# A two-layer sparse graph kernel: the last full block of the sorted rows goes without slots

## The chip, the cores and the metric

The kernel runs on one core of a Trainium2 chip. The metric is the device time of one execution in microseconds (us), the median of several runs. A profile is one execution recorded by the hardware profiler; its times are counted from the first instruction. Five engines work side by side, each through its own queue in order: TensorE (PE; its weight loads are listed as PEld), VectorE (DVE), ScalarE (ACT), GpSimd (POOL) and SyncE (SP). In this kernel GpSimd issues the gathers and scatters of rows, SyncE the plain loads.

## The reference

There are 2708 nodes with 1024 features in f32 and an adjacency matrix of zeros and ones, which is sparse: a node has few neighbours, and the expected number falls with the node's index.

```python
# layer 0: attention over the neighbours
q = x @ W_q.T + b_q;  k = x @ W_k.T + b_k;  v = x @ W_v.T + b_v
z = (q @ k.T) / sqrt(1024) * adj
z = where(z == 0, -10000, z)
x1 = layernorm(x + relu(softmax(z, axis=1) @ v))
# layer 1: a sum over the neighbours
out = layernorm(x1 + adj @ (x1 @ weight) + bias)
```

Two consequences matter here. A row without neighbours has all its scores at -10000, so its softmax is uniform and its attention output is the mean of v over all nodes, the same row for every such node. And in layer 1 such a row gets no neighbour sum: its output is layernorm(x1 + bias).

## The kernel before, in words

The kernel never forms the dense products. With M = W_q.T W_k it computes y = x M once per node (`y_block`), so that a score is a dot product of a y row with an x row. Since the rows of softmax sum to one, softmax @ v is (softmax @ x) @ W_v.T + b_v: for every row the kernel gathers its neighbours' x rows, mixes them into one row r, and multiplies r by W_v. Layer 1 does the same with x1 and `weight`. A small flag at the end says whether a row had more neighbours than its block has room for; if so, a dense path follows that computes everything again.

Rows are sorted by their number of neighbours, in two families (the first 1024 nodes and the other 1684), and cut into 22 blocks of 128 rows: blocks 0 to 7 and 8 to 21. Block 21 has only 20 rows. `SLOTS` says how many neighbours a block has room for: block 20 has one, block 21 none. Block 0 shares its work with a "hub" of extra slots. Blocks with one slot (18, 19, 20, the list `single`) go through `attend_one`: a mean row from `mean_rows` is overwritten by the one neighbour where there is one (L890), and a second piece of the job computes the score for the flag. The other blocks go through `attend`, one score (L813) and one accumulation (L870) per slot. Blocks with no slot are in `last`; they need no r, and `project_mean` multiplies the mean of x by W_v.

Layer 0 runs by a written list `steps`: "y" steps (y of one block), "v" steps (the projection of one block, `project`, L739) and "p" steps (the projection of two blocks as a pair). A pair is cut into quarters and done in seven half-size products instead of eight (`pair_products`, L999): VectorE builds four sums of the transposed blocks (`turn_pair`, L988 to L991) and evacuates partial results (L1011), and four differences of the weight quarters (L1136 to L1139) are made in place before the first pair. Before a product the rows r are transposed on TensorE (`flip`, L716) and copied by ScalarE (L717). After it, `finish0` or `finish_pair` adds the residual x, normalizes and scatters the rows to x1 (L703).

What VectorE works on meanwhile comes from the lists `jobs` and `late_jobs`: a planner keeps a credit in microseconds and runs the next job when there is credit, when a coming step needs its rows, or while block 0 is still in the list from step 15 on. Late jobs, those of the second family and block 7, wait until all y are done. Three buffers hold rows r.

Layer 1 runs over `units`. Its order of code is: turn the next unit's rows (`turn1`), fetch its residuals (`gather_x1`: ScalarE copies the bias into an xr buffer, L1251, and a gather adds x1 rows to it), issue the row gathers of the unit three ahead (`sum_rows`, L349 on GpSimd, L1238 and L1241 on VectorE), then the products (`work1`). The first unit, (20,), is a single block; the other ten are pairs. After unit 2 the blocks in `last` are fetched and finished without a product, by `finish1` with half sums on ScalarE (L1260). The xr buffers number three for the first block of a unit and the blocks in `last`, two for the second blocks. Before the first product the differences of the layer's weight quarters are made (L1304 to L1307).

The tile framework orders each engine's queue by priority, which follows the order of the code unless a block of code is marked urgent, and by readiness in its own model; the engine then works through that queue in order.

Of the kernel before, what the change touches and what calls it, by code (L numbers as in the profile page):

```python
# [20 lines left out]
P = 128  # L21
# [4 lines left out]
HUB = 32  # L26
# [4 lines left out]

SLOTS = [15, 11, 8, 6, 5, 4, 3, 2] + [13, 5, 4, 4, 3, 3, 3, 2, 2, 2, 1, 1, 1, 0]
ALONE = [8]
# [47 lines left out]
def sparse_part(ctx, tc, x, xT, adj, wqT, wkT, wvT, bq, bk, bv, w1, b1, out):  # L81
    nc = tc.nc
# [28 lines left out]
    with es:  # L111
# [608 lines left out]
        def flip_shares(shares, rT=None):  # L720
# [11 lines left out]
            return rT  # L732

        def project(rT, w):
            po = []
# [9 lines left out]
        def project_mean(rT, w):  # L745

            acc = p_o.tile([P, HALF], F32, name="po")
            with tc.high_priority(URGENT):
# [8 lines left out]
            for h in range(NH):  # L757
                acc = p_o.tile([P, HALF], F32, name="po")
                for g in range(h * G // NH, (h + 1) * G // NH):
                    k = g * D // G - h * HALF  # L760
                    put = nc.tensor.matmul(acc[:HUB, k:k + D // G], ident[:, g * HUB:(g + 1) * HUB], quarters,
                                           start=True, stop=True)
                po.append(acc)
            products.append(put)
            return po

# [296 lines left out]
        def finish_pair(pair, ts):  # L1063
            for k, (b, t) in enumerate(zip(pair, ts)):
# [9 lines left out]
                else:  # L1074
# [9 lines left out]
        jobs = [6, 5, 4, 3, 2, 2, 1, 1, "hub", "hub", 0, 0, 0]  # L1084
        pairs = [(7, 20), (19, 18), (17, 8), (16, 11), (15, 10), (9, 14), (13, 12)]
        late_jobs = [7, 20, 8, 19, 18, 8, 17, 8, 16, 11, 15, 10, 20, 9, 14, 19, 13, 12, 18]
        late = set(late_jobs)
        jobs, late_jobs = jobs + late_jobs, len(late_jobs)
        steps = [("y", 8), ("y", 9), ("y", 10), ("y", 11), ("y", 12), ("v", 6), ("y", 13), ("v", 5), ("y", 14), ("v", 4), ("y", 15), ("v", 3),
                 ("y", 16), ("v", 2), ("y", 17), ("y", 18), ("y", 19), ("y", 20), ("y", 21)]  # L1090
        steps += [("v", b) for b in [1, 0] + last] + [("p", pair) for pair in pairs]

# [14 lines left out]

        def turn0(b):
            if b in last:
                rT = hp.tile([P, DC, HUB], F32, name="mean", tag="y0T")  # L1110
                nc.scalar.copy(rT, xbT.unsqueeze(2).to_broadcast([P, DC, HUB]))
                return rT
# [6 lines left out]
        for i, (kind, b) in enumerate(steps):  # L1119
# [20 lines left out]
            for c in [c for st in steps[i:i + 3] for c in blocks_of(st) if not (left_y and c in late)]:  # L1140
                while c not in done0 and c not in got and c != 0:
                    credit -= run_job()
            while 0 in jobs and i >= 15:
                credit -= run_job()
# [75 lines left out]

        units = [(20,), (19, 18), (17, 16), (15, 1), (14, 2), (7, 8), (9, 3), (4, 10), (6, 0), (5, 11), (12, 13)]
        assert sorted(last + [b for unit in units for b in unit]) == list(range(NB))
# [421 lines left out]
```

## Time and profile before

| What | us |
|---|---|
| time before, median of 3 runs | 1066.83 (1064.39 to 1071.95) |
| profiled execution, from its first to its last instruction | 1065.8 |
| TensorE busy in it | 1007.5 |
| VectorE busy in it | 850.6 |
| GpSimd busy in it | 493.0 |
| ScalarE busy in it | 425.4 |
| end of the last product of layer 0 | 748.9 |
| first transposes of layer 1 | 760.7 |
| end of the last product of layer 1 | 1048.5 |

The profiled execution's time is given by its span alone, and it lies among the three timed runs. A line such as `L999 PE MATMUL po<-w,rT 128*128 128x512 f32 x8` reads: line 999 of the kernel, TensorE, a matmul that writes tile po from w and rT, a 128 by 128 stationary operand and 512 moving columns, eight records. Behind a row stands the time that the engine stood idle before it and what released it. Busy time of TensorE is modelled by the profiler and consecutive matmuls overlap, so starts are a better ruler than lengths.

### The profile page before, as it was taken

Reading aid. Unit: us, or ns where it says so; the run is one execution under the profiler, and the core shown is the slowest. Engines: PE = TensorE matmul, PEld = TensorE weight load, DVE = VectorE, ACT = ScalarE, POOL = GpSimd, SP = SyncE. Lnnn points to the kernel's source line nnn. Section 1 sums busy time; section 2 is a strip of 40 time slices with the busy share of each in tenths; the row PEclk is TensorE's granted clock in tenths of the full one; section 3 lists DMA queues with packets and bytes.
Section 4 is the critical chain, followed back from the end, with each engine's and each line's share of the span. In section 5 each row is a group of like instructions: output and inputs, shape, how many; then the busy total and the mean of one; then the engine's idle time right before and its main releaser. Section 6 shows DMA issues by size and latency. Waiting matters only on the chain.

```text
span 1065.8 us, 10216 instructions
## 1 busy us (share of the span) xinstructions
PE 1007.5 (95%) x2849; PEld 475.1 (45%) x2849; DVE 850.6 (80%) x1831; ACT 425.4 (40%) x894; POOL 493.0 (46%) x397
## 2 busy tenths in 40 slices
PE   7999999999988999999999999999589999999993
PEld 6444444444443444444545444444334444454441
DVE  8799999995287879999399999974678878896432
ACT  4688788422042332224424344332422363333321
POOL 1000140057654545526166666611577777787300
PEclk9999999999999999999999999999799999999997
DMA  9555458565887656796533777726589689979701
GB/s 363 184 205 204 167 207 290 160 216 168 292 250 253 200 181 203 236 331 201 175 114 96 239 247 258 260 95 210 151 286 262 201 274 324 282 221 323 192 40 42
DMA packets 90963, 229.20 MB, mean 215 GB/s; under 512 B 18411, under 2 KB 40395, under 8 KB 88189
## 3 DMA queue, kind: packets, MB, share of 16 engines
q0 software_dynamic: 48768, 148.05, 43.5%
q1 hardware_dynamic: 42128, 80.41, 21.9%
q8 instruction: 24, 0.39, 0.2%
q14 instruction: 43, 0.34, 0.1%
HBM read 219.61 MB, written 33.68 MB: 238 GB/s over the span
## 4 chain that ended last, share of the span: by engine, by line
PE 24%; DVE 12%; issue 5%; DMA 5%; POOL 3%; ACT 1%; POOLq 0%; DVEq 0%; ACTq 0%
PE po L999 21%; DVE r L870 3%; DMA g<-x_d,tabs 3%; DVE junkv L813 3%; DVE t L1011 1%; DMA yg<-y_d,tabs 1%; POOL g L349 1%; POOL xr L343 1%; PE tr L716 1%; PE po L739 1%; PE tr L729 1%; ACT junks L775 1%; DVE t L1069 1%; DVE r L1241 1%; DMA out_dram<-xr,tabs 0%
## 5 line engine op out<-in xcount | busy, mean ns | idle before, releaser
L319 PE MATMUL po<-m_sb,xt 128*128 128x512 f32 x672 | 292.1, 593 | 3.9 <-DVE yo L323 3.9
L319 PEld LDWEIGHTS po<-m_sb,xt 128*128 128x128 f32 x672 | 126.4, 190 | 160.1 <-issue 151.9
L813 DVE SCALAR_TENSOR_TENSOR junkv<-yg,g 128x1024 uint8<-128x1024 f32 x109 | 133.0, 1220 | 34.1 <-DMA g<-in_x_dram,tabs 16.7
L349 POOL DMA_INDIRECT g<-in_x_dram,tabs x86 | 110.7, 1288 | 72.3 <-DVE r L870 20.4
L999 PE MATMUL po<-t,s_all 128*128 128x512 f32 x272 | 124.3, 600 | 2.7 <-DVE xr L1011 2.7
L1241 DVE SCALAR_TENSOR_TENSOR r<-g,valid,r 128x1024 f32<-128x1024 f32 x77 | 98.6, 1281 | 19.1 <-DMA g<-x_d,tabs 18.3
L609 PE MATMUL po<-wk_o,wq_o 128*128 128x512 f32 x256 | 110.5, 592 | 0.0
L739 PE MATMUL po<-wv,rT 128*128 128x512 f32 x224 | 99.4, 602 | 3.6 <-DVE pr L855 3.0
L775 ACT ACTIVATE junks<-t,lnm 128x1024 uint8<-128x1024 f32 (+1 forms) x41 | 47.0, 1147 | 123.7 <-DVE lnm L773 95.2
L349 POOL DMA_INDIRECT g<-x_d,tabs x67 | 77.6, 1158 | 22.7 <-issue 12.8
L563 POOL DMA_INDIRECT tab_d<-rec,pos_i x22 | 27.1, 1230 | 130.0 <-DVE pos_i L552 123.6
L870 DVE SCALAR_TENSOR_TENSOR r<-g,pr,r 128x1024 f32<-128x1024 f32 x64 | 81.8, 1279 | 5.9 <-ACT r L882 4.6
L999 PE MATMUL po<-w,rT 128*128 128x512 f32 x192 | 86.4, 599 | 0.0
L332 ACT ACTIVATE junka<-xt 128x128 f32<-128x128 f32 x176 | 53.8, 306 | 76.1 <-PE po L319 57.5
L999 PEld LDWEIGHTS po<-t,s_all 128*128 128x128 f32 x272 | 51.9, 192 | 68.5 <-issue 61.9
L788 ACT ACTIVATE t<-t,nmr,rstd 128x1024 f32<-128x1024 f32 (+1 forms) x41 | 50.0, 1237 | 81.2 <-DVE nmr L787 81.0
L224 DVE MAX8 few<-a 128x8 f32<-128x75 f32 (+3 forms) x132 | 79.2, 618 | 0.0
L609 PEld LDWEIGHTS po<-wk_o,wq_o 128*128 128x128 f32 x256 | 48.3, 190 | 59.3 <-issue 59.1
L999 PE MATMUL po<-w,s_all 128*128 128x512 f32 x160 | 72.1, 592 | 0.0
L221 DVE SCALAR_TENSOR_TENSOR a<-a,iota 128x2708 f32<-128x2708 f32 (+1 forms) x22 | 65.2, 2963 | 5.4 <-ACT junk L220 5.4
L739 PEld LDWEIGHTS po<-wv,rT 128*128 128x128 f32 x224 | 42.8, 193 | 57.6 <-issue 56.8
L717 ACT COPY rT<-tr 128x512 f32<-128x512 f32 x80 | 43.1, 586 | 56.1 <-PE tr L716 56.1
(350 smaller groups left out, 1524.6 us busy)
## 6 DMA issues: line engine op xcount, KB each, us to landing
a<-in_adj_dram SPq DMA_DIRECT2D x21, 1354.0 KB, 5.9
xt<-in_xT_dram SPq DMA_DIRECT2D x21, 512.0 KB, 5.2
y_d<-yo SPq DMA_DIRECT2D x21, 512.0 KB, 6.1
g<-in_x_dram SPq DMA_DIRECT2D x21, 512.0 KB, 8.0
wq_i<-in_wqT_dram SPq DMA_DIRECT2D x8, 512.0 KB, 8.7
wk_i<-in_wkT_dram SPq DMA_DIRECT2D x8, 512.0 KB, 10.9
wv<-in_wvT_dram SPq DMA_DIRECT2D x16, 256.0 KB, 6.0
w<-in_w_dram SPq DMA_DIRECT2D x4, 1024.0 KB, 7.8
```

The source lines that it names most:

```text
L221: nc.vector.scalar_tensor_tensor(a[:n], a[:n], 1.0, iota[:n], op0=ALU.is_equal, op1=ALU.mult)
L224: nc.vector.max(few[:n, i * 8:(i + 1) * 8], a[:n, cuts[i]:cuts[i + 1]])
L319: put = nc.tensor.matmul(po, xt[:, c, :], m_sb[c // 2][:, c % 2, k0:k1], start=(c == 0), stop=(c == DC - 1))
L332: put = nc.scalar.activation(junka, xts[b][:, c, :], AF.Copy, accum_out=xs[:, c, b:b + 1])
L349: nc.gpsimd.indirect_dma_start(out=dst[:n], out_offset=None, in_=src, in_offset=bass.IndirectOffsetOnAxis(ap=at, axis=0), bounds_check=N - ...
L609: nc.tensor.matmul(po, wq_o[i // 2][:, o, i % 2 * P:(i % 2 + 1) * P], wk_o[:, o, hs], start=(o == 0), stop=(o == DC - 1))
L739: put = nc.tensor.matmul(acc, rT[:, c, :], w[c // 4][h][:, c % 4, :], start=(c == 0), stop=(c == DC - 1))
L775: nc.scalar.activation(junks[:n], t[:n], AF.Square, bias=nm[:n], accum_out=vs[:n])
L813: nc.vector.scalar_tensor_tensor(junkv[:n], yg[:n, :D], scale, xg[:n], op0=ALU.mult, op1=ALU.mult, accum_out=s)
L870: nc.vector.scalar_tensor_tensor(r[:n], xg[j][:n], pr[:n, j:j + 1], r[:n], op0=ALU.mult, op1=ALU.add)
L999: put = nc.tensor.matmul(acc, a[:, k], w[:, k], start=start and k == 0, stop=stop and k == DC // 2 - 1, skip_group_check=True)
L1241: put = nc.vector.scalar_tensor_tensor(r[:n], xg[:n], ok[:n, j:j + 1], r[:n], op0=ALU.mult, op1=ALU.add)
```

## The change

Block 20 gets no slot and joins block 21 in `last`. In layer 0 both take their rows from one product of the mean: `project_mean` now spreads the mean over all 128 partitions instead of 32, and the second call returns the same banks. Block 1, which had a "v" step of its own, takes block 20's place in the pairs: the first pair is (1, 19) and the second (7, 18). The job list loses block 20's two pieces, and the jobs of block 0 are forced one step earlier, since its projection is now the first "v" step after the y's. In layer 1 the unit (20,) goes, ten pairs stay, and both blocks 20 and 21 are finished after unit 2 without a product.

```diff
-SLOTS = [15, 11, 8, 6, 5, 4, 3, 2] + [13, 5, 4, 4, 3, 3, 3, 2, 2, 2, 1, 1, 1, 0]
+SLOTS = [15, 11, 8, 6, 5, 4, 3, 2] + [13, 5, 4, 4, 3, 3, 3, 2, 2, 2, 1, 1, 0, 0]
...
+        mean_po = []
...
         def project_mean(rT, w):
+            if mean_po:
+                return mean_po[0]
...
-                    put = nc.tensor.matmul(acc[:HUB, k:k + D // G], ident[:, g * HUB:(g + 1) * HUB], quarters,
+                    put = nc.tensor.matmul(acc[:, k:k + D // G], ident[:, g * HUB:g * HUB + 1].to_broadcast([P, P]), quarters,
                                            start=True, stop=True)
                 po.append(acc)
             products.append(put)
+            mean_po.append(po)
             return po
...
-        pairs = [(7, 20), (19, 18), (17, 8), (16, 11), (15, 10), (9, 14), (13, 12)]
-        late_jobs = [7, 20, 8, 19, 18, 8, 17, 8, 16, 11, 15, 10, 20, 9, 14, 19, 13, 12, 18]
+        pairs = [(1, 19), (7, 18), (17, 8), (16, 11), (15, 10), (9, 14), (13, 12)]
+        late_jobs = [19, 7, 8, 18, 8, 17, 8, 16, 11, 15, 10, 9, 14, 19, 13, 12, 18]
...
-        steps += [("v", b) for b in [1, 0] + last] + [("p", pair) for pair in pairs]
+        steps += [("v", b) for b in [0] + last] + [("p", pair) for pair in pairs]
...
         def turn0(b):
+            if b in last[1:]:
+                return None
...
-            while 0 in jobs and i >= 15:
+            while 0 in jobs and i >= 14:
                 credit -= run_job()
...
-        units = [(20,), (19, 18), (17, 16), (15, 1), (14, 2), (7, 8), (9, 3), (4, 10), (6, 0), (5, 11), (12, 13)]
+        units = [(19, 18), (17, 16), (15, 1), (14, 2), (7, 8), (9, 3), (4, 10), (6, 0), (5, 11), (12, 13)]
```

## The prediction

> **What bounds the kernel now.** First the page's head and busy times: TensorE is busy 95% of the span, VectorE 80%.
>
> ```profile
> span 1065.8 us, 10216 instructions
> PE 1007.5 (95%) x2849; PEld 475.1 (45%) x2849; DVE 850.6 (80%) x1831; ACT 425.4 (40%) x894; POOL 493.0 (46%) x397
> ```
>
> A share over the whole span hides the stages, so I cut the span where TensorE's work changes: 523 to 565 single blocks of layer 0, 565 to 749 its seven pairs, 749 to 784 the change of layers with the single unit of block 20, 784 to 1049 the ten pairs of layer 1. Columns: busy us of each engine, granted clock, DMA share, GB/s.
>
> ```profile
> 523.00:565.00 42.00, 41.45 (x208) 22.47 (x207) 35.09 (x62) 17.15 (x39) 19.59 (x14) 1.00 0.38 118
> 565.00:749.00 184.00, 180.28 (x488) 83.38 (x485) 158.33 (x365) 68.98 (x129) 94.86 (x68) 1.00 0.62 203
> 749.00:784.00 35.00, 21.45 (x74) 12.10 (x74) 21.16 (x27) 11.29 (x17) 23.91 (x17) 0.80 0.69 187
> 784.00:1049.00 265.00, 260.02 (x713) 122.48 (x711) 189.15 (x342) 93.96 (x160) 171.43 (x137) 0.99 0.74 232
> 540.00:703.00 163.00, 159.48 (x504) 74.73 (x503) 159.95 (x333) 63.15 (x119) 99.29 (x70) 1.00 0.59 195
> ```
>
> TensorE hardly stands still in either pair stage, but from 540 to 703 VectorE is as full (159.95 of 163). Then TensorE's timeline across the change of layers (start, length, line, what, count, idle before):
>
> ```profile
> 745.31 3.60 PE L999 MATMUL po<-t,rT 128*128 128x512 f32 x8
> 760.69 1.94 PE L716 MATMUL tr<-ident,r 128*128 128x128 f32 x8 [11.67 <-DVE r L1238]
> 762.46 2.07 PE L999 MATMUL po<-w,rT 128*128 128x512 f32 x2
> 767.54 13.04 PE L999 MATMUL po<-w,rT 128*128 128x512 f32 x30
> 782.99 1.06 PE L716 MATMUL tr<-ident,r 128*128 128x128 f32 x8 [1.54 <-DVE r L1241]
> 783.89 7.03 PE L999 MATMUL po<-w,rT 128*128 128x512 f32 x16
> 793.59 5.40 PE L999 MATMUL po<-t,s_all 128*128 128x512 f32 x8 [2.67 <-DVE xr L1011]
> ```
>
> Two records make one f32 matmul of the code, and groups of 8 start 3.43 us apart, so 0.429 us a record: a block alone is 16 matmuls = 32 records = 13.7 us, a pair 56 records = 24.0 us, and 8 transposes 0.9 us (590.47 to 591.34). Block 20 alone fills 762.5 to 780.4. Last the chain of waits where the small last block is finished in layer 1:
>
> ```profile
> 861.80 4.99 DMA out_dram<-xr,tabs
> 866.87 1.04 ACT xr L1251
> 869.86 0.66 PE tr L716 x4
> ```
>
> A residual buffer xr comes free only when the last block's scatter has landed; ScalarE's next copy stands in its queue behind that, the copies of turned rows behind it, and TensorE loses 1.63 us.
>
> **What the Trainium skill says.** "TensorE: Matmul & The Clock Gate", Part 1: an idle window of about 3.4 us halves the array's clock, and about 3.4 us of work restores it. The trace agrees: after the 11.67 us gap the granted clock is 0.53 from 761 to 767, 1.00 after. "SBUF — State Buffer", Who interferes with whom: a VectorE instruction with two SBUF inputs contends with GpSimd reads. The trace fits: beside the weight differences the xr gathers at 761.71 and 766.85 took 2.55 and 3.22 us, 1.16 at 679.51 without such a neighbour. "Perfetto Trace Analysis", Identifying the Most-Contended Engine: matmul busy time is a poor measure; hence I count start-to-start.
>
> **Part by part.**
>
> *Layer 0, TensorE.* Pairs stay seven: block 1 takes 20's place. Block 1's own step goes: 32 x 0.429 = 13.7 us; of transposes one block's net, 0.9 us. The mean's first product stays (64 records, 3.6 us). Its spreading keeps 8 records of 256 columns (1.91 us), with full instead of narrow outputs; weight loads may grow from 106 to 190 ns, 8 x 0.08 = 0.7 us at most and beside the matmuls, so I take 0. The second last block reuses the banks. Sum: -14.6 us.
>
> *Layer 0, the others.* Gone for block 20: one score (1.22 + 0.08), the mask (0.2), one accumulation (1.28), so 2.8 us of VectorE; a mean-row copy (1.15) and one block's turned copies (2 x 0.59) of ScalarE; three GpSimd gathers (some 1.3 us each), not its xr gather nor its scatter. A step of two adds, a relu-sum and a norm is only exchanged between blocks 1 and 20: 0. Block 1's row buffer, one of three, is held longer; VectorE has enough else to do, so 0, at most one row stream of 3 us.
>
> What is late next is VectorE. The last turned rows are ready at 703.2 and their pair starts at 724.7; block 8's are ready at 605.4, and its pair starts at 617.6, where the first 6.9 us need the partner alone. TensorE comes 14.6 us sooner, VectorE's row work only 2.8, minus the evacuations of half a pair more (about 5 us) that now fall before it. So block 8 is late by about 14.6 - 12.2 - 6.9 + 2.2 + 4 = 2 us, the 4 being its transposes, copies and sums. The four weight differences (L1136 to L1139, 2.2 us each) now meet the finishing of three blocks, about 2 us; and block 19's result buffer waits for block 0's scatter, 0 to 3 us, with VectorE's queue behind that add. I take 4 us of new stalls in all, bounds 0 and 11.8 (nothing but VectorE's 2.8 is gained). The third job of block 0 is issued a step sooner, but VectorE is full there (39.8 of 40 us in 460 to 500) and the work the same: 0, within 2 us either way. Layer 0: **-10.6** (between -14.6 and -2.8).
>
> *Change of layers.* The 11.67 us gap stays: the last scatter and the first gathers do not change. Then unit (19, 18) is first: block 19's transposes take block 20's place at 760.7, block 18's rows block 19's place (landed by 763.2); the first two products need block 19 alone, so with 3.8 us of transposes at the slow clock the products start by about 764.5. Its products started at 783.9: 19.4 us removed, of which 13.7 are block 20's products. What they covered comes out: the differences L1304 to L1307 are 4 x 2.2 = 8.9 us and the four sums 2.7 us, of which two differences and two sums must precede the third product. From 760.5 that is about 5.8 us of VectorE plus the wait for rows, against 7 to 8 us of products at the half clock. The residual is asked for later in GpSimd's queue, behind six row gathers at 1.3 us instead of three: from 757.6 it is issued at 766 and lands 5.7 later at 772, and one more add goes before the third product: about 2 us. The old stall in that place was 2.67 and falls away with that pair's old position, so I charge 2.
>
> *Layer 1, row gathers.* GpSimd issues all the time (14 per 20 us) and loses one gather, 1.3 us; block 20's moved no rows. If TensorE is some 18 us sooner, do rows arrive? Rows ready against start of their pair: (15, 1) 803.6 and 840.1; (14, 2) 825.7 and 865; (7, 8) 855.9 and 893; (9, 3) 884.6 and 919; (4, 10) 904.9 and 945; (6, 0) 956.0 and 975.9; (5, 11) 975.7 and 1000. Only (6, 0), with the hub, has under 20: 19.9 less 5 for its transposes, so 18 - 1.3 - 15 = about 2 us of stall.
>
> *Layer 1, the zero blocks.* Block 20 now ends like 21: a bias copy (1.05), two half sums (2 x 0.80), a norm on ScalarE, a gather and a scatter. The sums are new, 1.6 us of ScalarE beside matmuls; VectorE drops 2 x 0.77 + 0.69 + 0.75. But 20 and 21 take two of three xr buffers, so a unit's residual can be asked for only as its forerunner's leaves or block 20's scatter lands. Copy 1.05 + issue 1.5 + landing 5.7 = 8.3 us against 6.9 us until the third product needs it: 1.4, and for the next unit again; GpSimd's and ScalarE's queues stand behind those waits as at 866.87. I take 4, bounds -1.6 (the present stall gone) and 12. Layer 1: -19.4 + 2 + 2 + 4 = **-11.4**.
>
> **Sum.** -10.6 - 11.4 = -22.0 on the profiled execution's 1065.8 us span gives 1043.8. Its time lies 1.0 below the median 1066.83; from the median it is **1045**.
>
> **Rivals.**
> - *Everything hidden.* No new stall: -14.6 - 19.4 = -34, 1033. For it: rows lie 20 to 40 us ahead. Against: VectorE full from 540 to 703. Chance 0.12.
> - *VectorE holds layer 0* and the xr buffers cost their worst: -2.8 - (19.4 - 4 - 8) = -10.2, 1057. For it: 98% busy there, four stalls of TensorE on row results in 673 to 704. Against: results come 20 us before their pair. Chance 0.19.
> - *The two zero blocks block layer 1.* If block 20's scatter stands in GpSimd's queue behind two units' row gathers (2 x 13 x 1.3 = 34 us), and the next unit's residual waits for it, that wait less 6 us of lead is 28; with 5 of landing it takes 33 out: 1045 + 33 = 1078. It decides against the change from a wait of 22 us. Against: the buffer of the forerunner comes free anyway. Chance 0.08.
> - *The change does not do what it says:* a row of block 20 with a neighbour would raise the flag and run the dense path, at least three projections of 22 blocks, 3 x 22 x 13.7 = 904 us more. In the reference's adjacency 164 of the last 1684 rows are empty and blocks 20 and 21 need 148. Chance 0.01.
>
> **How the numbers follow.** The forecast, 1045, gets 0.60, between 1037 and 1053. The range takes in both neighbours, 1032 to 1059. 1% is 10.7 us, about what a measurement here can tell from no change: under 1056.2 lie the forecast, the hidden case and a third of the VectorE case: 0.78; within 1% the rest of that case: 0.13; above it the two last: 0.09.
>
> **What would show it.** Right: the first pair of layer 0 starts near 551 instead of 565, the first pair products of layer 1 come 4 us after the first transposes, and TensorE's count falls from 2849 records to 2769 (64 of products, 16 of transposes). Wrong: TensorE idle before transposes on row accumulations (L870) above 12 us in the pair stage, waits for a scatter of xr above 10 us in layer 1, or matmuls queued behind transposes whose rows are not there.

## The result, and the profile after

The changed kernel takes 1076.73 us (median of four runs, 1073.67 to 1084.39), the kernel before, timed beside it, 1065.61 (1063.28 to 1071.95). The ratio is 1.010, 95% interval 1.0066 to 1.0134: about 1% slower, where 1045 and a gain of 2% were forecast. The time lies above the range (1032 to 1059).

The head and busy times of the changed kernel's page, which answer the first lines of the prediction:

```profile
span 1071.9 us, 10026 instructions
PE 987.5 (92%) x2769; PEld 467.0 (44%) x2769; DVE 842.8 (79%) x1820; ACT 422.9 (39%) x893; POOL 493.0 (46%) x393
```

TensorE has 2769 records, the number forecast, and 20 us less of busy time. The work is gone; the time is not. The span is 6.1 us longer, so TensorE is 26 us longer not busy. (The profiled run of the changed kernel is the fastest of its four, so the span shows less of the loss than the medians.)

TensorE's timeline of the changed kernel, its stalls over 1.5 us behind 504 (start, length, line, what, count, idle before and what ended it). Lines have moved by a few: L1004 is the old L999, L1016 the old L1011, L875 the old L870, L1245 and L1248 the old L1238 and L1241, L1258 the old L1251.

```profile
504.97 2.43 PE L319 MATMUL po<-m_sb,xt 128*128 128x512 f32 x4 [2.48 <-DMA xt<-in_xT_dram]
...
570.38 2.84 PE L1004 MATMUL po<-wv,s_all 128*128 128x512 f32 x6 [1.70 <-DVE lnm L776]
575.50 3.70 PE L1004 MATMUL po<-t,s_all 128*128 128x512 f32 x8 [2.28 <-DVE t L1016]
594.95 1.94 PE L716 MATMUL tr<-ident,r 128*128 128x128 f32 x8 [6.29 <-DVE r L875]
...
760.85 1.94 PE L716 MATMUL tr<-ident,r 128*128 128x128 f32 x8 [13.85 <-DVE r L1245]
...
839.00 6.28 PE L1004 MATMUL po<-t,s_all 128*128 128x512 f32 x8 [4.98 <-DVE xr L1016]
892.29 5.24 PE L1004 MATMUL po<-t,s_all 128*128 128x512 f32 x8 [4.16 <-DVE rstd L790]
960.96 0.60 PE L729 MATMUL tr<-to_h,part 128*128 128x32 f32 x2 [9.57 <-DVE part L1248]
```

Of these only the one at the change of layers was there before (11.67 us). Before, the stage up to the pairs had no wait for a slab, the pairs of layer 0 no stall over 1.3 us, and TensorE reached the transposes of block 0, in the unit that also carries the hub, without a pause:

```profile
955.35 1.02 PE L999 MATMUL po<-w,rT 128*128 128x512 f32 x2
956.21 0.40 PE L729 MATMUL tr<-to,r 128*128 128x96 f32 x2
```

VectorE's last accumulation for that unit ended at 956.1:

```profile
953.49 2.60 DVE L1241 SCALAR_TENSOR_TENSOR r<-g,valid,r 128x1024 f32<-128x1024 f32 x2
```

The slack was 0.1 us: TensorE and the rows came level. Behind the new stall the clock is low too: the small transposes of the hub start 0.85 us apart instead of 0.45. "TensorE: Matmul & The Clock Gate", Part 1, of the Trainium skill says that an idle window of about 3.4 us halves the clock; 9.57 us of idleness and these starts agree. The low clock lasts longer than the 3.4 us of work that the prediction took from the same page: the granted clock is 0.50 up to 969 and 1.00 from 971, so it takes some 9 us here, and it took about 6 us after the change of layers.

The windows of the layer-1 stage, from the first row gather to those transposes, in the kernel before and in the changed one (length, busy us and count of each engine, granted clock, DMA share, GB/s):

```profile
757.60:956.40 198.80, 189.43 (x528) 90.91 (x529) 161.16 (x252) 69.48 (x119) 157.18 (x123) 0.97 0.83 257
```

```profile
755.60:960.90 205.30, 179.68 (x488) 84.81 (x488) 158.05 (x250) 71.70 (x123) 159.25 (x122) 0.93 0.81 249
```

Read the fifth pair, GpSimd. Between two of its DMA issues lie 0.30 us, so before it spends 157.2 + 123 x 0.30 = 194.1 of 198.8 us issuing, and after 159.3 + 122 x 0.30 = 195.9 of 205.3. Its queue is full in this stage in both kernels, though the whole span shows it 46% busy; the rest is 4.7 us of waits before and 9.4 after. In GpSimd's account 4.7 us more of waits and 1.8 of issue, net, make up the 6.5 us by which the stage grew. "Perfetto Trace Analysis", What "DMA-bound" means, of the Trainium skill has the case: the sequencer track of the issuing engine is solid with DMA slices. The trace agrees once the 0.30 us between the slices are counted; only, it shows in this stage and not in the share of the whole span.

GpSimd's timeline of the changed kernel, where its queue waits and where the hub's rows are fetched:

```profile
895.35 0.91 POOL L703 DMA_INDIRECT out_dram<-xr,tabs  x1 [4.88 <-ACT xr L793]
...
913.32 0.99 POOL L349 DMA_INDIRECT g<-x_d,tab  x1 [0.30 <-issue]
...
935.08 1.02 POOL L349 DMA_INDIRECT g<-x_d,tab_h  x1 [0.30 <-issue]
...
956.68 1.63 POOL L343 DMA_INDIRECT xr<-x_d,tabs  x1 [0.31 <-issue]
```

Block 0's 15 gathers by `tab` and the hub's 11 by `tab_h` run from 913 to 954 without a residual gather (L343) between. In the kernel before the hub's ran from 898 to 913, then came two scatters, two residual gathers and three gathers for block 6, then block 0's.

VectorE and ScalarE of the changed kernel, the waits at the head of their queues, and VectorE's last six accumulations for the hub:

```profile
569.63 0.69 DVE L1016 TENSOR_TENSOR t<-po,bias_bc 128x512 f32<-128x512 f32 x1 [4.71 <-DMA x_d<-t,tabs]
...
831.27 2.48 DVE L1248 SCALAR_TENSOR_TENSOR r<-g,valid,r 128x1024 f32<-128x1024 f32 x2 [5.48 <-DMA g<-x_d,tabs]
...
889.55 1.28 DVE L1248 SCALAR_TENSOR_TENSOR r<-g,valid,r 128x1024 f32<-128x1024 f32 x1 [3.87 <-DMA g<-x_d,tabs]
...
918.88 1.28 DVE L1248 SCALAR_TENSOR_TENSOR r<-g,valid,r 128x1024 f32<-128x1024 f32 x1 [2.32 <-DMA g<-x_d,tabs]
...
952.93 7.88 DVE L1248 SCALAR_TENSOR_TENSOR part<-g,valid_h,part 128x1024 f32<-128x1024 f32 x6
```

```profile
892.85 1.04 ACT L1258 COPY xr<-bias 128x1024 f32<-128x1024 f32 x1 [3.42 <-DMA out_dram<-xr,tabs]
```

The waits of VectorE for gathered rows at 831 and 889 stand in front of TensorE's stalls at 839 and 892. From 918.9 to 960.8 VectorE then has no idle time over 0.4 us: it adds up block 0's rows and the hub's in one run of 42 us. In the kernel before, where the hub's had been done earlier, the last such run is 26 us long (930.0 to 956.1). So in the last 42 us GpSimd's gathers and VectorE's accumulations are both without slack, and the hub's rows need both.

So there are three places: the stage before 524, the pairs of layer 0 with the buffer wait at 569.6, and in layer 1 the rows of the unit with the hub, which come through GpSimd's queue and then VectorE's. In the profiled runs, from the first projected block to the end of y the change adds 2.7 us; from there to the first pair it takes 15.6; the pair stage grows by 12.5; layer 1, from its first gather to its last product, by 9.2. With -1.6 from ahead of these, -1.1 in the tail and rounding at the seams that is +6.1. The medians differ by 11.

### The profile page after: what moved, and what is told of

Same layout as the page of the kernel before. It is cut to its first block, busy times and chain, and to the rows that moved or that the text cites. A ratio compares the mean times of both kernels' runs of the same rounds, so it can differ in the third digit from the quotient of the medians.

```text
span 1071.9 us, 10026 instructions
## 1 busy us (share of the span) xinstructions
PE 987.5 (92%) x2769; PEld 467.0 (44%) x2769; DVE 842.8 (79%) x1820; ACT 422.9 (39%) x893; POOL 493.0 (46%) x393
## 4 chain that ended last, share of the span: by engine, by line
DVE 38%; PE 18%; issue 18%; DMA 14%; POOL 9%; ACT 2%; POOLq 0%; DVEq 0%
PE po L1004 13%; DVE a L221 6%; DVE few L224 6%; DVE junkv L818 5%; DMA g<-in_x_dram,tabs 4%; POOL g L349 3%; DVE r L875 3%; DMA g<-x_d,tabs 3%; DVE t L1016 2%; DVE r L1248 2%; PE po L319 1%; DMA r<-x_d,tabs 1%; DMA xt<-in_xT_dram 1%; POOL tab_d L563 1%; POOL xr L343 1%
## 5 line engine op out<-in xcount | busy, mean ns | idle before, releaser
L1004 PE MATMUL po<-t,s_all 128*128 128x512 f32 x272 | 129.0, 617 | 11.5 <-DVE xr L1016 5.0
L1248 DVE SCALAR_TENSOR_TENSOR r<-g,valid,r 128x1024 f32<-128x1024 f32 x77 | 98.0, 1279 | 19.2 <-DMA g<-x_d,tabs 18.6
L1004 PEld LDWEIGHTS po<-t,s_all 128*128 128x128 f32 x272 | 53.1, 199 | 80.8 <-issue 62.0
L741 PE MATMUL po<-wv,rT 128*128 128x512 f32 x192 | 83.7, 593 | 2.1 <-DVE pr L860 2.1
L875 DVE SCALAR_TENSOR_TENSOR r<-g,pr,r 128x1024 f32<-128x1024 f32 x64 | 81.7, 1277 | 0.9 <-ACT r L873 0.6
L1004 PE MATMUL po<-w,rT 128*128 128x512 f32 x160 | 73.3, 600 | 0.2 <-DVE t L1285 0.2
L1004 PE MATMUL po<-w,s_all 128*128 128x512 f32 x160 | 72.4, 593 | 0.3 <-DVE xr L1016 0.3
L219 ACT ACTIVATE junk<-a 128x2708 uint8<-128x2708 f32 (+1 forms) x22 | 54.1, 2459 | 24.3 <-DMA a<-in_adj_dram 19.7
```

What stands on the lines that cost most here:

```text
L219: nc.scalar.activation(junk[:n], a[:n], AF.Sign, accum_out=cnt[:n, b:b + 1])
L741: put = nc.tensor.matmul(acc, rT[:, c, :], w[c // 4][h][:, c % 4, :], start=(c == 0), stop=(c == DC - 1))
L875: nc.vector.scalar_tensor_tensor(r[:n], xg[j][:n], pr[:n, j:j + 1], r[:n], op0=ALU.mult, op1=ALU.add)
L1004: put = nc.tensor.matmul(acc, a[:, k], w[:, k], start=start and k == 0, stop=stop and k == DC // 2 - 1, skip_group_check=True)
L1248: put = nc.vector.scalar_tensor_tensor(r[:n], xg[:n], ok[:n, j:j + 1], r[:n], op0=ALU.mult, op1=ALU.add)
```

## The experiments

The runs came from chips on which the kernel before took between 1068 and 1080 us, so each ratio is to the kernel before timed beside it, and stage lengths are taken within each profile. Each stage length is of one execution; two runs that leave layer 1 as it was have C of 292.9 and 293.8, so 2 or 3 us of C mean little. The theory at the outset: streams of rows (VectorE's in layer 0, GpSimd's gathers in layer 1) set the ends, and the change delays them by waits for buffers. The rival: TensorE's work sets the end, and only the order in its queue loses it. A, first projected block to the end of y; B, first pair to the last product of layer 0; C, first gather to last product of layer 1, all in us:

| Kernel | A | B | C | time to before (95%) |
|---|---|---|---|---|
| before | 188.2 | 183.5 | 290.9 | 1 |
| changed | 190.9 | 196.0 | 300.1 | 1.0100 (1.0066 to 1.0134) |
| changed layer 0 alone | 194.4 | 197.4 | 293.8 | 1.0035 (1.0009 to 1.0060) |
| changed layer 1 alone | 187.6 | 183.3 | 300.3 | 1.0067 (1.0048 to 1.0086) |
| changed, four result buffers | 191.7 | 190.8 | 299.7 | 1.0006 (0.9980 to 1.0032) |
| changed, own buffer for block 20 | 190.5 | 195.9 | 302.7 | 1.0100 (1.0029 to 1.0171) |
| changed, zero blocks late | 189.8 | 195.5 | 292.6 | 0.9975 (0.9955 to 0.9994) |
| changed, block 6's transposes behind | 189.2 | 197.1 | 300.8 | 1.0082 (1.0050 to 1.0115) |
| changed, hub's transposes behind | 192.9 | 196.0 | 305.1 | 1.0109 (1.0071 to 1.0147) |
| before, 5 hub gathers | 186.9 | 183.1 | 299.4 | 1.0025 (1.0001 to 1.0048) |
| changed, 5 hub gathers | 190.7 | 196.0 | 293.0 | 0.9983 (0.9966 to 1.0000) |
| changed, zero blocks late, four buffers | 194.9 | 191.2 | 289.9 | 0.9933 (0.9908 to 0.9957) |
| the same, hub's unit last | 192.9 | 191.2 | 279.3 | 0.9841 (0.9809 to 0.9873) |
| before, the same three edits | 187.0 | 183.3 | 300.0 | 1.0086 (1.0066 to 1.0107) |
| before, block 0's jobs a step sooner | 191.6 | 183.3 | 292.9 | 1.0026 (1.0010 to 1.0042) |
| changed, constant loads sooner | 204.8 | 197.5 | 303.3 | 1.0206 (1.0173 to 1.0240) |
| three edits and constant loads sooner | 205.6 | 191.2 | 282.3 | 0.9964 (0.9946 to 0.9981) |
| before, zero block late, four buffers | 187.0 | 183.3 | 296.8 | 1.0059 (1.0034 to 1.0084) |
| changed, hub's gathers a unit sooner | 190.3 | 195.8 | 302.5 | 1.0068 (1.0054 to 1.0082) |
| before, hub's gathers a unit later | 186.5 | 183.4 | 298.0 | 1.0034 (1.0011 to 1.0057) |

### Each layer alone

```diff
 # changed kernel: layer 1 keeps the unit
-        units = [(19, 18), (17, 16), ...
+        units = [(20,), (19, 18), (17, 16), ...
 # kernel before: layer 1 drops it; block 20 is finished with block 21
-        units = [(20,), (19, 18), (17, 16), ...
+        units = [(19, 18), (17, 16), ...
-                for b in last:
+                for b in [20] + last:
```

> The changed layer 0, with layer 1 as it was (block 20 keeps its own unit with a one-slot gather, and is not finished with block 21). Stream theory (the rows' way through VectorE sets the end of layer 0, since the last transposes stand in TensorE's queue where the rows get ready): layer 0 ends about 2 us sooner, layer 1 is as before, 1064 us, that is 0.996 to 1.000 of the time before. TensorE theory (work taken off TensorE counts, the loss comes from layer 1's order): 10 us off, about 1055. VectorE's wait for block 0's scatter (4.7 us) and TensorE's stalls in front of late rows are still there.

> The kernel before with its layer 0, and of the change only that block 20 has no unit in layer 1 and is finished beside block 21. Stream theory: the hub's rows set layer 1, the first pair starts 20 us sooner and then waits; the rows come some 6 us later through the buffer waits, so 1075 us (1.005 to 1.012 of the time before). TensorE theory: 11 us off as forecast, about 1055. If the two halves of the change only hurt together, this one is within 2 us of before.

Neither half gains: 1.0035 and 1.0067. They add up to the changed kernel's 1.010, so nothing shows that the halves hurt each other; each loses by itself. Layer 1 alone falls where the stream theory put it (1.005 to 1.012). Layer 0 alone is worse than either theory said: its pair stage B behaves as expected, but A takes 194.4 us. That place nobody had named; it comes back below.

### Layer 0: a fourth result buffer

```diff
-            t = xb_pools[0].tile([P, D], F32, name="t", bufs=3) if b in [0] + last else ...
+            t = xb_pools[0].tile([P, D], F32, name="t", bufs=4) if b in [0] + last else ...
-            ts = [(xb_pools[0] if k else wp).tile([P, D], F32, name="t", bufs=2 + k) for k in range(2)]
+            ts = [(xb_pools[0] if k else wp).tile([P, D], F32, name="t", bufs=2 + 2 * k) for k in range(2)]
```

> The changed kernel with four result buffers of the second blocks of pairs in layer 0 where there are three, so that block 19's result no longer waits for block 0's scatter. Stream theory: VectorE's 4.7 us wait at 570 goes, its rows come 4.7 us sooner, about 1072 (4 to 5 us under the changed kernel). If VectorE's busy time or the gathers bound it whatever the buffers, no change: 1077.

B falls from 196.0 to 190.8, by 5.2, and the two stalls at 570 and 575 are gone. The time falls by 9 parts in a thousand of before, 10 us; B accounts for 5 us of it. On top of another edit (zero blocks late, below) the same buffers take off 4 parts, 4.5 us, which is B's size, so the rest is likely no more than what the intervals leave open. The result buffer did bind: while VectorE waits for it, all rows behind it are late. One stall stays, in TensorE's timeline of this kernel:

```profile
602.01 1.94 PE L716 MATMUL tr<-ident,r 128*128 128x128 f32 x8 [6.03 <-DVE r L875]
```

VectorE has no idle time over 0.04 us in this kernel from 552 to 603, nor in the kernel before from 544 to 592. Without the buffer wait it is VectorE's own work that keeps the rows: TensorE starts its pairs 15 us sooner and meets rows that come at VectorE's pace. From the end of y to the last product of layer 0 it is 225.5 us before, 222.4 changed and 217.3 here, so 8.2 of the 15.6 us saved in front of the pairs are kept once the buffer is there.

### Layer 1: a buffer of its own for block 20

```diff
-            xr = (cp if k else wp).tile([P, D], F32, name="xr", bufs=2 if k else 3)
+            xr = wp.tile([P, D], F32, name="xr0", bufs=1) if b == last[0] else \
+                (cp if k else wp).tile([P, D], F32, name="xr", bufs=2 if k else 3)
```

> The changed kernel with a residual buffer of its own for block 20 in layer 1, so that the next units' residual copies no longer wait for its scatter. Stream theory: ScalarE's 3.4 us and GpSimd's 4.9 us waits at 890 go, the hub's rows are ready about 4 to 5 us sooner, about 1072. If the gathers themselves (their bytes, VectorE's accumulations) set the hub's end, no change: 1077. Were the zero blocks the whole cause, the time would fall below that of before, 1065.

The stream theory missed: 1.0100, and C no shorter. (The interval of this run is wide, 1.0029 to 1.0171; it is the trace that decides.) GpSimd's and ScalarE's timelines of this kernel say why:

```profile
901.12 1.02 POOL L703 DMA_INDIRECT out_dram<-xr,tabs  x1 [1.99 <-ACT xr L793]
...
909.82 1.61 POOL L703 DMA_INDIRECT out_dram<-xr,tabs  x1 [3.77 <-ACT xr L793]
```

```profile
894.07 0.63 ACT L1268 ACTIVATE junks<-xr 128x512 uint8<-128x512 f32 x1 [3.71 <-DMA xr<-x_d,tabs]
```

The wait for the buffer went, and GpSimd waits 1.99 and 3.77 us at the two scatters of the zero blocks instead, since ScalarE's norm in front of them waits for the blocks' own residuals. What costs is, by this trace, not the buffer but a scatter that stands in GpSimd's queue before its rows are ready. The theory was changed to that: GpSimd's in-order queue paces layer 1, by its items and by each wait at its head.

### Layer 1: the zero blocks behind the row gathers

```diff
-            if i == 2:
+            if i == 8:
                 for b in last:
                     pending.append((b, gather_x1(b), None))
```

> The changed kernel with the two zero blocks of layer 1 finished behind the ninth unit instead of the third, so that their two residual gathers and two scatters come after all row gathers in GpSimd's queue. GpSimd theory (its in-order queue of gathers, one every 1.6 us without a pause from 757 to 957, sets when the hub's rows are there, and every wait at its head moves them): 4 items x 1.6 = 6.4 us and the 4.9 us wait for ScalarE's norm go from in front of the hub, so from the first gather to the hub's transposes 194 us instead of 205, and the time is about 11 us under the changed kernel, that is at or just under the kernel before (0.998 to 1.002). If VectorE's accumulations or the bytes set the hub's rows, no change: 1.010.

0.9975: 13 us under the changed kernel, and just under the kernel before. The window of the same stage in this kernel:

```profile
766.40:963.40 197.00, 177.52 (x488) 83.66 (x488) 155.61 (x240) 62.43 (x103) 150.37 (x118) 0.96 0.81 253
```

205.3 has become 197.0, not the 194 expected: four items fewer and shorter issues take 10.1 us from GpSimd (8.9 of busy time, 1.2 of gaps), and its waits grow by 1.8 net: a row gather waits 3.8 us at 813.6 and a scatter 3.7 us at 907.7, neither of which the changed kernel has. Part of this gain is not an undoing: block 21's two items stood ahead of the hub in the kernel before as well.

VectorE tells the gathers' part from its own. Its last run without idle time begins here at

```profile
921.28 1.28 DVE L1248 SCALAR_TENSOR_TENSOR r<-g,valid,r 128x1024 f32<-128x1024 f32 x1 [3.23 <-DMA g<-x_d,tabs]
```

and is 42 us long, as in the changed kernel. Counted from the first gather of layer 1 it begins after 154.8 us instead of 163.2, and these 8.4 us are the gain of the stage. So GpSimd's queue sets when the run begins, and VectorE's work how long it lasts.

### The hub's gathers cut, in both kernels

```diff
-            for j in range(tab.shape[1] if b else J0):
+            for j in range((5 if b == "hub" else tab.shape[1]) if b else J0):
```

> The kernel before with 5 of the hub's 11 row gathers in layer 1 (6 gathers and their accumulations, a part of the neighbour sum of the hub's rows, are left out). GpSimd theory: in the kernel before the hub's rows come 0.2 us before TensorE gets to their transposes, so TensorE and GpSimd are level there; 6 x 1.7 = 10 us off GpSimd's queue lets TensorE start nothing sooner: within 2 us of before (0.998 to 1.001). If the kernel before was bound by the gathers already, 8 to 10 us off: 0.991.

> The changed kernel with 5 of the hub's 11 row gathers in layer 1 (6 gathers and their accumulations, a part of the neighbour sum of the hub's rows, are left out). GpSimd theory: the hub's rows come 10 us sooner, the 9.6 us stall and the slow clock behind it (3 us) go, about 11 us under the changed kernel: 0.998 to 1.002 of before. If the loss lies in the stalls ahead of it (at 839 and 892) and the hub's stall only takes up what they left, the gain is under 4 us: 1.006 or more.

The same six gathers left out gain 12 us in the changed kernel and nothing in the kernel before (1.0025). So fewer rows for the hub let TensorE go on sooner after the change, and did not before it. The pair does not say which engine held the rows, since six accumulations of VectorE go with the gathers. The traces do: in the changed kernel VectorE's last run begins no sooner (165.6 us after the first gather, against 163.2) but is 8.1 us shorter (33.8 instead of 41.9), so there it is VectorE's work that was saved. In the kernel before, the hub's accumulations lie outside the last run, and that unit's rows are ready 197.5 us after the first gather instead of 198.5. The kernel before even loses 0.25%: it shows a new stall of 4.8 us near 860, whose cause was not followed, so its "nothing" may hide a few us.

### Is it only TensorE's order?

```diff
 # first try: turn1 of the unit with block 0 is emitted behind work1 of the unit before
 # second try: the same, and
-                        nc.tensor.matmul(tr[:, k, at:at + n], r[:, c * P:(c + 1) * P], to, ...)
+                        put = nc.tensor.matmul(tr[:, k, at:at + n], r[:, c * P:(c + 1) * P], to, ...)
+                        if after is not None:
+                            follow(put, after, same=True)
+                            after = None
-... flip_shares([(part, to_h), (r, to_0)], rT) if b == 0 ...
+... flip_shares([(part, to_h), (r, to_0)], rT, products[-1]) if b == 0 ...
```

> The changed kernel with the transposes of the unit that holds block 0 and the hub put behind the products of the unit before it, not in their midst. Order theory (TensorE has products left that it could do while the hub's rows are awaited; only its in-order queue keeps it from them): the 9.6 us stall at the hub's transposes shrinks to 3 us or less, and the time falls by 6 to 10 us, to 1.000 to 1.004 of before. If the hub's rows are needed at once anyway (the products left are too few), no change: 1.010.

> The changed kernel with the hub's and block 0's transposes tied behind the last product of the unit before (the edit before it moved only block 6's). GpSimd's queue is as in the changed kernel, so the hub's rows come 205 us after the first gather as before. Order theory: the four products of unit (4, 10) left at the stall, 13.7 us, run meanwhile, the stall is gone and the time falls by 8 to 13 us, to 0.998 to 1.003 of before. If those products hang on VectorE's evacuations, which stand behind the hub's accumulations in VectorE's queue, TensorE waits for these instead and the gain is under 4 us: 1.006 to 1.010.

The first try decides nothing: in the order it left, only block 6's transposes had moved, the hub's stood where they were. The second did place the hub's behind the last product of unit (4, 10), and is no faster (1.0109). TensorE and VectorE of it (L1007 and L1019 are the changed kernel's L1004 and L1016):

```profile
969.73 5.25 PE L1007 MATMUL po<-t,s_all 128*128 128x512 f32 x8 [8.68 <-DVE xr L1019]
```

```profile
968.99 0.69 DVE L1019 TENSOR_TENSOR xr<-po,xr 128x512 f32<-128x512 f32 x1 [2.69 <-DMA xr<-x_d,tabs]
```

TensorE now waits 8.68 us for the evacuation of unit (4, 10), and that one first for the hub's accumulations in VectorE's queue, then for a residual which GpSimd issues only behind the hub's gathers. The products that seemed free to go ahead hang on the same queue. The rival falls, for this place.

### Several causes together, and a version that beats both

> The changed kernel with the zero blocks finished late and with four result buffers, both together. If the two causes are separate stages (5.2 us in layer 0, 8.3 us up to the hub in layer 1), the gains add: 13 us in layer stages plus some 2 of slow clock under the changed kernel, 0.992 to 0.995 of before. If layer 0 ending sooner only makes layer 1 wait more, no more than the zero blocks alone: 0.9975.

> The same with the unit that holds block 0 and the hub as the last of layer 1 (the hub's gathers stay where they are in GpSimd's queue). If the hub's rows are what TensorE waits for, the 4.4 us stall and the slow clock behind it go too: 6 to 9 us more, 0.985 to 0.989. If another unit's rows are then late in the same way (GpSimd's queue is full until 987), the stall moves and the gain is under 3 us: 0.990 to 0.994.

> The kernel before with the same three edits (four result buffers, the zero block finished late, the hub's unit last) and none of the change: block 20 keeps its product. GpSimd theory: the kernel before has no stall at the hub, so the edits buy it little, 0 to 4 us: 0.996 to 1.000. Then what the changed kernel gains over it with the same edits, some 10 us, is what the products removed are worth once the queues don't hold them back. If the edits are worth as much here, the change is worth nothing: 0.986 to 0.990.

> The kernel before with four result buffers and its one zero block finished late, the hub's unit in its old place. If the waits they remove belong to the change (the kernel before shows neither a result buffer's wait nor a stall at the hub): within 3 us of before, 0.997 to 1.001. If they are worth as much here as in the changed kernel (18 us together): 0.984.

```diff
-        units = [..., (4, 10), (6, 0), (5, 11), (12, 13)]
+        units = [..., (4, 10), (5, 11), (12, 13), (6, 0)]
```

By the stages the two edits add: B 191.2, C 289.9. The time, 0.9933, is as forecast; the sum of the two single gains would have been 0.988, a difference which the intervals just about leave open. Moving the hub's unit to the end makes it 0.9841, 1051.26 us against 1068.84 beside it. In layer 1 of that kernel TensorE's stall at the hub is gone, and none over 0.7 us is left behind 840; the window of the whole stage C:

```profile
753.60:1032.90 279.30, 267.13 (x744) 127.48 (x744) 201.02 (x351) 99.56 (x171) 192.45 (x151) 0.98 0.77 238
```

C is 279.3 us instead of 300.1. The kernel before with the same three edits is slower than without (1.0086), and with two of them as well (1.0059), both against the forecast of no change; its zero block was finished behind the last unit but one, as in the changed kernel. So the edits don't help by themselves; they help where products have been taken out. What the products removed are worth once the rows keep up can be read from the two fastest orders found: 1.6% between the kernel before and the changed one with three edits. No order was sought for the kernel before, so this may be too much. Why the kernel before loses by the edits was not followed up: its layer 1 shows new waits, 4.0 us for a copy of turned rows near 873 in one, 2.7 and 2.2 near 936 and 973 in the other.

### Stage A: block 0's jobs a step sooner

In every run with the changed layer 0 as it is, TensorE waits between 1.3 and 5.4 us for an input slab or, once, a score between 504 and 524; no run with the old one unchanged waits over 1.1 us there. One line of the change reaches that place.

```diff
 # kernel before
-            while 0 in jobs and i >= 15:
+            while 0 in jobs and i >= 14:
 # changed kernel
-                if b == NB - 5:
+                if b == NB - 6:
                     row_constants(1)
```

> The kernel before with one edit of the change alone: block 0's remaining jobs are dealt at step 14 instead of step 15. If the shift costs what the changed kernels lose near 510: the 13 row-constant loads start near 468 instead of 454, TensorE waits 2 to 5 us for the slab that stands behind them, 1.002 to 1.005 of before. If the shift is free as predicted: 0.999 to 1.001, and the loss there comes from block 1's missing step.

> The changed kernel with the 13 row-constant loads one step sooner, so that they stand ahead of block 0's last jobs again. If the shift costs it: the wait near 505 goes and the time falls by 3 to 5 us under the changed kernel, to 1.005 to 1.007 of before. If layer 0's pairs, which wait for VectorE's rows anyway, take the gain back: no change, 1.010.

> The changed kernel with four edits: four result buffers, zero blocks finished late, the hub's unit last, and the 13 loads one step sooner. If the four causes are separate: 3 to 5 us under the kernel with three edits (0.984), that is 0.979 to 0.981 of before, the 20 us once forecast. If the wait near 507 only hides another wait: 0.984.

The step alone costs the kernel before 0.26%, 2.8 us, as the first theory said. SyncE's queue before and with the step (13 loads of L681, then a slab of L280):

```profile
453.73 8.36 SPq L681 DMA_DIRECT2D g<-in_x_dram  x4
462.57 0.38 SPq L280 DMA_DIRECT2D xt<-in_xT_dram  x1
...
465.33 9.77 SPq L681 DMA_DIRECT2D g<-in_x_dram  x9
```

```profile
480.21 21.48 SPq L681 DMA_DIRECT2D g<-in_x_dram  x13
501.79 0.38 SPq L280 DMA_DIRECT2D xt<-in_xT_dram  x1
```

Dealt a step sooner, block 0's jobs stand ahead of the 13 row-constant loads, which then start late and run in one piece just ahead of the next slab; this chip was 9 us later at the first projected block, so of the 26 us between the two starts 17 are the shift. TensorE then waits 3.44 us at 524.6 for the last slab. Which of the reordered items holds that slab was not followed further. The remedy tried is worse than the loss: with the loads in front, block 0's maxima come late and TensorE stands 15.3 us before their transposes at 515.2. Both kernels with that edit pay it. The four edits together are slower than three: 0.9964 against 0.9841. So the line that costs was found, and no better place for it.

### The hub's place in the list of units

```diff
 # changed kernel: 3 instead of 4; kernel before: 5 instead of 4
-            if i == 4:
+            if i == 3:
                 sum_rows("hub")
```

> The changed kernel with the hub's gathers emitted one unit sooner, as they stood against the other units in the kernel before. If the shift of the hub makes the loss of layer 1: the stall of 9.6 us at the hub's transposes falls under 5 us, 4 to 8 us under the changed kernel, 1.003 to 1.006 of before. If only the number of items and the waits in front of the last row of unit (6, 0) count, which this doesn't change: block 0's rows are late in the hub's place, 205 us after the first gather, and the time is the same, 1.010.

> The kernel before with the hub's gathers emitted one unit later, which is the shift that dropping a unit brings, and nothing else of the change. If the shift makes the loss of layer 1: a stall of some 4 us or more at the hub's transposes and 1.004 to 1.008 of before. If only the number of items and waits in front counts: within 2 us, 0.998 to 1.002.

The hub's gathers are emitted at the fifth place in the list. Dropping the first unit moves them a unit later against all others, which the change does not show and the prediction did not see. The shift alone costs the kernel before 0.34%, 3.6 us; undoing it in the changed kernel brings 1.0100 to 1.0068, 3.4 us, with intervals that touch. By the times about half of layer 1's 0.67% may be the shift, but neither number is sharp, and both runs differ from what was forecast. In the kernel before no stall over 0.8 us appears at the hub's transposes; waits of 2.2 and 3.1 us do, near 833 and 921. In the changed kernel the stall did not vanish: of the 9.6 us at the hub 2.6 stay, two waits of 2.1 and 2.8 us appear in front, and C is no shorter (302.7).

The rows say more. By the shift alone VectorE's last run in the kernel before grows to 44.8 us and the unit's rows are ready 206.0 us after the first gather instead of 198.5; in the changed kernel it is 205.2. So the shift is enough to make the rows as late as they are. TensorE, with block 20's products still to do, comes there as late itself and loses little. Undoing the shift is not enough: in the changed kernel the last gather of the unit is still issued as late (196.8 us after the first, against 196.6), and VectorE waits for TensorE in between, so the rows come after 207.7. The shift undone together with the zero blocks late was not run.

## Why the prediction was wrong

*Work removed.* Right: 80 TensorE records fewer, 20 us of busy time, the first pair of layer 0 at 550.9 (551 forecast), the first pair's products of layer 1 within 4 us of the first transposes. The arithmetic of what goes was right. What it is worth was not.

*Change of layers, "I charge 2".* Right in size: the third product of the first pair starts at 775.3 instead of 793.6, 18.3 us sooner, where 17.4 follow from the sum. But "the 11.67 us gap stays" did not hold. It is 13.85 us: the first gather is now block 19's, and its rows are there 4.3 us after the issue, those of block 20's after 2.2. The gap is 13.75 with layer 1 changed alone and 11.71 with layer 0 alone, so it belongs to layer 1, and it takes back what layer 0 had gained.

*Layer 1, row gathers, "about 2 us of stall".* The step that failed first. Slack was measured from when a unit's rows are ready to when its pair of products starts (956.0 against 975.9), less 5 us for transposes. But the transposes stand in TensorE's queue in the midst of the products of the unit before, at 956.2. Slack was 0.1 us, and more than TensorE had gained up to there was lost: 18.3 us ahead at 775, it was 5 us behind at these transposes, with waits of 4.98, 4.16 and 9.57 us and the low clock behind them. GpSimd's line, "14 per 20 us", was read as a price of one gather, not as a queue that was full for 199 us, and VectorE's accumulations behind it were not counted.

*Layer 1, zero blocks, "I take 4".* The waits were of the size taken (4.88 us on GpSimd, 3.42 on ScalarE). They were charged to buffers; a buffer of its own brought no gain, a later place for the scatters gained 13 us. The mechanism was the queue that they stand in, which sets when the hub's rows can be begun.

*Layer 0, "4 us of new stalls".* The pair stage grew by 12.5 us. Block 19's buffer wait, given 0 to 3 us, measured 4.71, and was worth 5.2. The rest, some 7 us, is VectorE without idle time. The bound named for this, nothing gained but VectorE's 2.8, comes near the number, since layer 0 ended 2.0 us sooner, but that is luck: 1.6 of it lie ahead of the first projected block, and the rest is 15.6 saved less 12.5 in the pairs and 2.7 in stage A.

*The third job of block 0, "0, within 2 us either way".* It costs 2.8 us in the kernel before (1.1 to 4.5 by the interval), through loads in SyncE's queue that were not among the things it was moved past in the working.

*Not in the sum at all:* the shift of the hub's gathers, which by itself makes the rows of that unit late.

*Signs.* Of the three signs of being wrong one showed, matmuls queued behind transposes whose rows are not there. The idle time before layer 0's transposes (6.29 us the longest) and the wait for a scatter of xr (3.42) stayed under what was named.

*Rivals.* "VectorE holds layer 0" named the right engine; that its size fits is luck, as said. "The two zero blocks block layer 1" named the time within 2 us (1078) and the engine, but by a wait of 28 us behind row gathers; the measured one is 4.9 us, so the number is luck. "Everything hidden" did not come true, and with 2769 records of TensorE, as counted beforehand, the dense path did not run.

## What to carry to other kernels

Where two engines are both near full in a stage, removing work from one can turn another into the bound: compute each queue's items plus gaps in that stage before counting the gain. Measure slack at the place where the consumer stands in its static queue, not where its result is used. And when an item leaves a list, look at everything placed by index in that list, and at what is waiting at the head of each in-order queue.

## What the runs showed of the hardware

A residual gather that adds to its target kept GpSimd 1.87 us on the mean (16 of them in layer 1 of the kernel before), a plain row gather 1.19, each with 0.30 us to the next. The prediction took 1.5 and 1.3. Its comparison of the adding gathers at 761.71 and 766.85 with 1.16 us at 679.51 mixes two kinds, since that one is a plain gather of layer 0.

The price of an issue is not fixed. The hub's gathers took 1.09 us each in the kernel before and 1.40 in the changed one, block 0's 1.32 and 1.15: dear is whichever comes second. What differs is VectorE beside them. In layer 1 of all 20 traces 639 row gathers ran with no VectorE instruction beside them that reads two SBUF tiles (an accumulation, a sum or a weight difference), and they took 0.99 to 1.05 us; every longer one, up to 2.83 us, had such a neighbour, though not every neighbour made one longer. GpSimd and VectorE of the changed kernel:

```profile
758.29 0.99 POOL L349 DMA_INDIRECT g<-x_d,tabs  x1 [0.30 <-issue]
...
761.13 2.64 POOL L349 DMA_INDIRECT r<-x_d,tabs  x1 [0.30 <-issue]
```

```profile
760.62 2.28 DVE L1311 TENSOR_TENSOR w<-w,w 128x2048 f32<-128x2048 f32 x1
```

This is the contention that the prediction named beside the weight differences. It reaches further: VectorE's accumulations slow the very gathers that feed them.
